# Layer 0 of a state-space and convolution network on one core: another order of the first steps, other places for the silus, one ScalarE table set for ln and exp

## Chip, cores and metric

The kernel runs on one core of a Trainium2 chip. The core has TensorE (PE in the profile; PEld is its weight load), VectorE (DVE), ScalarE (ACT), GpSimd (POOL) and SyncE (SP), which here issues nearly all DMAs. The metric is the device time of one execution in microseconds, lower is better.

## What is computed

Input x is 4 images of 512 channels by 32 by 32 points, all in float32. Layer 0 is a selective state-space mixer over the 1024 points of each image taken as tokens; layer 1 is a block of 3x3 convolutions with a spatial attention map. Both sit behind a group norm and a residual sum.

```python
x = x + _L0(_gn(x), ...)
x = x + _L1(_gn(x), ...)

# layer 0
xn = (x - mu) / sqrt(var + 1e-05) * ln_w + ln_b
xm, z = split(xn @ W_in)                       # 1024 channels each
xs = silu(causal_conv4(xm) + conv_b)
proj = xs @ W_x
dt = softplus(proj[..., :32] @ W_dt + b_dt)
Bm, Cm = proj[..., 32:48], proj[..., 48:]
A = -exp(A_log)
h = exp(dt * A) * h + (dt * xs) * Bm           # along the tokens, 16 states
y = sum_s(h * Cm) + xs * D_param
out = (y * silu(z)) @ W_out
```

## The kernel before

**Layer 0** goes through the batches b = 0 to 3. The 1024 channels of the mixer are 8 tiles of 128 (NDC); tokens come in 2 halves of 512 (NH). One *group* is a pair of channel tiles (index e) and one half (h): 8 groups a batch, 32 in all. A group runs 16 *units* (`unit`), one for each state s: ScalarE computes the decay exp(dt A) (`decay`, L832, two of 128 x 512), the input term comes either from ScalarE row scalings that TensorE turns (L844, L870; nine states, `B_ON_ACT`) or from a GpSimd product (L859; seven states), VectorE runs the recurrence (`tensor_tensor_scan`, L884), the product with C is GpSimd's (L906) except for four states of VectorE's (L900), and TensorE adds the states up in PSUM (L913). A group is opened by `delta` (step size dt: matmul L394 `pd`, bias L779, softplus L785, product with x on GpSimd L793, transposes and copies L809) and closed by `gate` (copies of y L936, transposes back L946, D x and the product with silu(z) on VectorE L953 and L956, store to `gd`).

While batch b goes through its groups, the next batch is prepared beneath: `norms` (group norm and layer norm over channels; its square roots are made as exp(-0.5 ln v), L458 and L463 for the group norm, L550 and L556 for the layer norm, with squares at L532 and matmuls at L539), `conv1` (projection to xm in three parts, four taps on ScalarE and VectorE, L639 and L648, then a silu of the whole 128 x 1024 tile, L657), `params` (`proj`, with B and C to DRAM `bcd` and back as broadcast tiles `cbc` and `bbc`). `gates` projects z, copies it out of PSUM (L707), applies silu (L711, 128 x 1024) and stores it to DRAM `szd`; `gate` loads it back as `szl` (one buffer) four units before its group ends.

Batch 0 has a version by halves, `conv1_half`: the first half's eight channel tiles are projected and convolved, the three last columns of each are kept in `tails`, group 0 can then start, and the second half follows beneath it, with small instructions at L687 for the columns that straddle the halves.

A filler runs under all this: `transform`, 32 pieces that prepare the 3x3 weights of layer 1 (GpSimd L1173 to L1193, ScalarE L1165 and L1166, loads of 192 KB and stores of 128 KB by SyncE). Eleven of them (PRM `t0`) come with priority -190, the others every 21.42 units (`tg`).

**The order** of all instructions of layer 0 is worked out when the kernel is built. `Plan.step` records an engine, an estimated duration, what is read and written, a priority (`prio`, in units: group n of batch b starts at (8b + n) x 16) and the ScalarE function table that is needed (`table`). `Plan.issue` then simulates the five engines: for each it takes, of the steps that can start soonest, the one with the lowest priority number; a step that needs another table is charged `LOAD` = 1.3 us, and only entered early if no urgent step of the present table waits. Steps marked `fill` may run up to 17.64 units (`AHEAD`) ahead. Each engine then executes its instructions strictly in that order. ScalarE's function tables are loaded by an instruction of their own (`ACT_TABLE_LOAD` in the profile, listed under the line that needs it), which the compiler puts in.

**Layer 1** (from L1260 on in the program, 2045 us in the profile) is not touched, apart from one thing: its group norms (`rsqrt`, L255 and L256) also use ln and exp.

```python
PRM = dict(..., m0=45.7, n0=50.77, q0=65.56, qg=5.2, c0=61.67, cg=6.03, e0=3.46, eg=4.75, dl=10.28, t0=11, tg=21.42)
"xs": 10, "win": 2, "yt": 1, "dt": 2, "dtx": 2, "dtxt": 2, "cbc": 5,
"sc": 2, "h": 4, "sz": 1, "bb": 3, "dbx": 4, "szl": 1, "wpr": 2, "res": 2,
```

These are the priorities and the buffers of each ring that the text speaks of; PSUM has two buffers `mm`, four `u` and two `y` besides.

Of the kernel before, what the change touches and what calls it, by code (L numbers as in the profile page):

```python
# [15 lines left out]
P = 128  # L16
# [14 lines left out]
PRM = dict(pg=0.53, kt=2, ke=1, ka=-0.68, fl=0, fi=4.6, m0=45.7, n0=50.77, nl=2.05, q0=65.56, qg=5.2, c0=61.67, cg=6.03, p0=112, e0=3.46, eg=4.75, g0=78.98, gg=9.04, o0=13.03, og=5.23, dl=10.28, t0=11, tg=21.42)  # L31
# [24 lines left out]
class Plan:  # L56
# [7 lines left out]
    def __init__(self, slots, in_order):  # L64
        self.slots, self.steps = dict(slots), []
        self.queues = {r: [] for r in in_order}
# [37 lines left out]
    def issue(self):  # L104
# [6 lines left out]
        while left:  # L111
# [32 lines left out]
            s.fn()  # L144
            if late:
                t += self.LOAD
                table = s.table
            clock[s.eng] = t + s.us
# [21 lines left out]
def mamba_then_pab_kernel(  # L170
# [31 lines left out]

    gm_sb = cpool.tile([P, P], F32, tag="gmat", name="gm_sb")
# [70 lines left out]
    with ExitStack() as l0:  # L274
# [6 lines left out]

        NT = L // P
# [41 lines left out]
        tails = wp.tile([P, NDC, 3], F32, tag="tails", name="tails")  # L324
# [7 lines left out]
        def dram_set(name, shape, n=B):  # L332
# [14 lines left out]
            ("xt", "u", "h", "cbc", "bb", "dbx", "sc"),  # L347
# [31 lines left out]
        xts, ready, xs, xh, dts = {}, {}, {}, {}, {}  # L379
        pieces = buf(None, None, "")  # L380
        tail = [buf(None, None, "") for d in range(NDC)]
# [19 lines left out]
        def norms(b, prio, lag=0.0):  # L401

            t = xts[b] = buf("xt", [P, NCC, L], f"xt_{b}")
            src = x[b].rearrange("(c p) h w -> p c (h w)", p=P)
            xin = [buf(None, None, "") for c in range(NCC)]
            step("SP", 0.0, lambda: t(), [], [], prio, holds=[t])
            for c in range(NCC):
                step(
                    "SP", 0.3, lambda c=c: nc.sync.dma_start(t()[:, c, :], src[:, c, :]),
# [29 lines left out]
            def mid():  # L439
# [19 lines left out]
                [pv], [stat], prio, "ln",  # L459
# [42 lines left out]
            by_chunk = by_token(NCC)  # L502
            for h, hs in enumerate(halves):
                prio += lag
# [8 lines left out]
                    prio, holds=[t],  # L513
                )
                for c in range(NCC):
# [6 lines left out]
                        [pmu], [by_half[h]], prio, holds=[t],  # L522
                    )
            pvars = []
            for h, hs in enumerate(halves):
                prio += lag
                pvar = buf("mm", [P, T], f"pvar_{b}_{h}")
                for c in range(NCC):
                    sq = buf("res", [P, T], f"sq_{b}_{h}_{c}")
                    step(  # L530
                        "ACT", 0.61,
                        lambda c=c, hs=hs, sq=sq: nc.scalar.activation(  # L532
                            sq(), t()[:, c, hs], AF.Square, bias=spl["nb"][:, c : c + 1]
                        ),
                        [by_half[h], stat], [sq], prio, holds=[t],
# [86 lines left out]
        def tap_weights(d):  # L622
            return [cw_sb[:, 4 * d + 3 - k : 4 * d + 4 - k] for k in range(4)]
# [1032 lines left out]
```

## Time and profile before

| what | us |
|---|---|
| median of 3 runs (lowest, highest) | 3085.72 (3081.79, 3090.05) |
| the profiled execution: its time, its span | 3085.98, 3084.2 |
| busy in the span: TensorE, VectorE, ScalarE, GpSimd | 2760.5, 2325.2, 1864.1, 2181.5 |
| softplus of group 0, of group 1 | 105.5, 200.7 |
| ends of the groups of batch 0 (`yt` copy, L936) | 242, 301, 361, 418, 487, 552, 614, 667 |
| of batch 1 | 721, 778, 835, 895, 968, 1032, 1096, 1148 |
| of batch 2 | 1201, 1259, 1312, 1376, 1449, 1513, 1577, 1630 |
| of batch 3 | 1683, 1741, 1794, 1842, 1897, 1945, 1997, 2045 |

Times within an execution count from the first instruction. Batches 0 to 2 take some 480 us each from one end of the last group to the next, batch 3 takes 415; the first group of all ends at 242. Layer 1 begins at 2045 and fills the other third, with TensorE busy 968.3 of the last 994 us.

A row of a group of instructions gives line, engine, operation, output and inputs, shapes, the count, then busy time and the mean of one in ns, then the engine's idle time just before them with what ended it. In a row of busy time by window each engine's microseconds stand with its count of instructions; PEclk is TensorE's granted clock.

### The profile page before, as it was taken

How to read it: one execution, taken by the hardware profiler on the slowest of the kernel's cores; microseconds unless marked ns; L12 is line 12 of the kernel's file. 1: busy time of each engine (PE TensorE's matmuls, PEld its weight loads, DVE VectorE, ACT ScalarE, POOL GpSimd, SP SyncE). 2: the span in 40 equal slices, each digit the busy share in tenths (PEclk: the TensorE clock that was granted, in tenths of full speed). 3: DMA queues.
4: the chain of work that ended last, by engine and by line, in shares of the span. 5: the costliest groups of instructions: out<-in, count | busy, mean ns of one | idle time of the engine just before them, and what ended most of it. 6: DMA issues, size and time to landing. Idle time of an engine off the chain costs nothing. (4 is left out here: it accounts for less than half of the span.)

```text
span 3084.2 us, 36053 instructions
## 1 busy us (share of the span) xinstructions
PE 2760.5 (90%) x11512; PEld 1625.3 (53%) x11512; DVE 2325.2 (75%) x3021; ACT 1864.1 (60%) x3218; POOL 2181.5 (71%) x1221
## 2 busy tenths in 40 slices
PE   4788789999879999879999978779999999999998
PEld 2245556656656666656656656544444444444444
DVE  3567999989999988999999899986275375447344
ACT  4578899998789999779999787741120030021000
POOL 6899988899988899998899999862151142224222
PEclk8899899999989999988999999999999999999999
DMA  6776645578745567755557755638178448628827
GB/s 170 216 208 197 178 143 164 171 210 255 230 138 163 165 204 238 236 176 158 174 167 238 237 184 151 148 123 307 54 259 314 163 165 315 256 76 313 309 86 259
DMA packets 410292, 610.49 MB, mean 198 GB/s; under 512 B 47832, under 2 KB 246744, under 8 KB 385528
## 3 DMA queue, kind: packets, MB, share of 16 engines
q1 hardware_dynamic: 401296, 593.67, 61.1%
q10 hardware_dynamic: 8648, 14.26, 1.3%
q8 instruction: 92, 1.51, 0.2%
q14 instruction: 96, 0.79, 0.1%
q0 software_dynamic: 160, 0.26, 0.0%
HBM read 511.09 MB, written 96.99 MB: 197 GB/s over the span
## 5 line engine op out<-in xcount | busy, mean ns | idle before, releaser
L906 POOL TENSOR_TENSOR da<-da,cbc 128x1024 f32<-128x1024 f32 x288 | 680.6, 2370 | 80.4 <-DVE da L884 50.7
L844 ACT ACTIVATE sc<-dtxt,bt_sb 128x256 f32<-128x256 f32 x1152 | 506.6, 497 | 70.6 <-PE u L870 70.1
L859 POOL TENSOR_TENSOR dbx<-dtx,bbc 128x1024 f32<-128x1024 f32 x224 | 529.1, 2373 | 20.1 <-PE y L913 7.0
L832 ACT ACTIVATE da<-dt,a_sb 128x512 f32<-128x512 f32 x576 | 395.4, 712 | 45.7 <-PE y L913 42.9
L884 DVE TENSOR_TENSOR_SCAN da<-da,carry_sb,u 128x512 f32<-128x512 f32 x288 | 357.6, 1263 | 34.5 <-PE u L870 34.5
L870 PE MATMUL u<-ident,sc 128*128 128x128 f32 x2304 | 345.8, 284 | 41.1 <-DVE da L884 26.0
L913 PE MATMUL y<-ident,da 128*128 128x128 f32 x2304 | 317.3, 282 | 53.2 <-POOL da L906 50.7
L913 PEld LDWEIGHTS y<-ident,da 128*128 128x128 f32 x2304 | 269.3, 145 | 155.6 <-POOL da L906 104.5
L884 DVE TENSOR_TENSOR_SCAN da<-da,u 128x512 f32<-128x512 f32 x288 | 348.6, 1210 | 2.6 <-PE u L870 2.4
L1468 PE MATMUL m_b<-uw_b,v_b 128*128 128x512 f32 x768 | 336.3, 595 | 8.8 <-DMA uw_b<-u_b 7.7
L870 PEld LDWEIGHTS u<-ident,sc 128*128 128x128 f32 x2304 | 277.2, 146 | 122.8 <-DVE da L884 34.7
L1468 PE MATMUL m_o<-uw_o,v_o 128*128 128x512 f32 x768 | 334.2, 595 | 4.3 <-DVE v_o L1387 4.1
L832 ACT ACTIVATE u<-dt,a_sb 128x512 f32<-128x512 f32 x448 | 297.6, 680 | 47.3 <-DVE da L884 27.6
L913 PE MATMUL y<-ident,dbx 128*128 128x128 f32 x1792 | 267.8, 289 | 61.2 <-DVE dbx L900 31.0
L913 PEld LDWEIGHTS y<-ident,dbx 128*128 128x128 f32 x1792 | 219.2, 149 | 135.0 <-issue 48.0
L394 PE MATMUL pxm<-xt,winc 128*128 128x345 f32 (+3 forms) x704 | 249.4, 498 | 29.3 <-DMA winc<-in_w_in_dram 12.9
L394 PE MATMUL pz<-xt,winc 128*128 128x512 f32 x512 | 240.3, 601 | 8.4 <-ACT sz L707 2.1
L1468 PEld LDWEIGHTS m_b<-uw_b,v_b 128*128 128x128 f32 x768 | 143.2, 190 | 195.0 <-issue 174.5
L1468 PEld LDWEIGHTS m_o<-uw_o,v_o 128*128 128x128 f32 x768 | 145.3, 190 | 190.1 <-issue 181.3
L906 POOL TENSOR_TENSOR dbx<-dbx,cbc 128x1024 f32<-128x1024 f32 x96 | 227.2, 2366 | 15.5 <-DVE dbx L884 7.5
L1518 PE MATMUL pat<-y_b,st 128*128 128x512 f32 x512 | 221.7, 593 | 0.1
L1476 ACT ACTIVATE e_b<-m_b 128x512 f32<-128x512 f32 x24 | 14.3, 597 | 307.9 <-PE m_b L1468 306.3
(233 smaller groups left out, 4543.1 us busy)
## 6 DMA issues: line engine op xcount, KB each, us to landing
cbc<-bcd SPq DMA_DIRECT2D x512, 256.0 KB, 3.7
uw_b<-u_b SPq DMA_DIRECT2D x96, 1024.0 KB, 5.1
uw_o<-u_o SPq DMA_DIRECT2D x96, 1024.0 KB, 4.8
bbc<-bcd SPq DMA_DIRECT2D x224, 256.0 KB, 3.9
u_b<-work SPq DMA_DIRECT2D x192, 128.0 KB, 2.7
u_o<-work SPq DMA_DIRECT2D x192, 128.0 KB, 3.3
winc<-in_w_in_dram SPq DMA_DIRECT2D x72, 256.0 KB, 3.6
szd<-sz SPq DMA_DIRECT2D x32, 512.0 KB, 4.1
```

The costliest lines, as they stand in the source:

```text
L394: lambda k=k, lhs=lhs, rhs=rhs: nc.tensor.matmul(p()[:, at : at + cols], lhs(), rhs(), start=(k == 0), stop=(k == n - 1)),
L832: nc.scalar.activation(t, dt()[:, j], AF.Exp, scale=a_sb[:, at : at + 1])
L844: nc.scalar.activation(sc()[:, k], dtxt()[:, k], AF.Copy, scale=bt[:, at, s : s + 1])
L859: lambda: nc.gpsimd.tensor_mul(hc(), dtx(), b_bc().to_broadcast([P, 2, T])),
L870: nc.tensor.transpose(u()[:, k * P : (k + 1) * P], sc()[:, k, j, :], ident)
L884: nc.vector.tensor_tensor_scan(ht, *((hc()[:, j], u()) if on_act else (u(), hc()[:, j])), carry_sb[:, j, s : s + 1] if h else 0.0, ALU.mul ...
L906: lambda: nc.gpsimd.tensor_mul(hc(), hc(), c_bc().to_broadcast([P, 2, T])),
L913: nc.tensor.matmul(y[j]()[:, k, :], hc()[:, j, k * P : (k + 1) * P], ident, start=(s == 0 and k == 0), stop=(s == NS - 1 and k == NK - 1), ...
L1468: nc.tensor.matmul(m[q], v[:, q, k, c, :], w[:, c, :], start=(c == 0), stop=(c == NCC - 1 and not extra),)
L1476: nc.scalar.activation(e, m[2], AF.Copy, scale=al / 2)
L1518: nc.tensor.matmul(pt, st[m][:, 2 * P * j + h : 2 * P * (j + 1) : 2], xb[m // 2][:, m % 2, :], start=(m == 0), stop=(m == NMC - 1),)
```

## The change

- **Tables.** `exp_set`, a preload of the set `natural_log_exp_and_others`, is issued at the kernel's start and by the plan each time that ScalarE comes back to exp; steps of ln now carry the table name "exp".
- **silu of z.** `gates` no longer applies it; z is stored as projected. `load_gate` loads it 11.5 units (`zl`) before its group ends, instead of 4, and its silu (128 x 1024, over both tiles of the pair) is run by the *next* group's `delta`.
- **One ScalarE step.** `delta`'s softplus step first runs a list of jobs: the silu of the last group's z and, in groups 5, 6 and 7 of a batch, the silu of two x tiles of the next batch; then softplus. The last two x tiles of a batch have a step of their own (`alone`). `gate` is recorded after the next group's `delta` (`end_group`). TensorE's transposes in `gate` now also wait for the z tile.
- **First steps.** x of batch 0 is loaded ahead of the plan; its norm goes by halves (`at_half`), with the squares in the `dt` and `dtx` buffers instead of the two of `res`; `conv1_half` becomes `conv1_first`, which takes the second half in two parts of 256 columns and projects three columns again instead of keeping `tails`; its silus come for four tiles at once in the second half. Priorities: norm -60 to -20, first convolutions -26 to -17, transforms -190 to -5.
- **Numbers.** `t0` 11 to 7, `tg` 21.42 to 18.5, `dl` 10.28 to 8.5, `e0` 3.46 to 6, `m0` 45.7 to 48; batch 1's convolutions use the spacing of the other batches.

```diff
-PRM = dict(..., m0=45.7, ..., q0=65.56, qg=5.2, ..., e0=3.46, ..., dl=10.28, t0=11, tg=21.42)
+PRM = dict(..., m0=48, ..., e0=6, ..., dl=8.5, t0=7, tg=18.5, zl=11.5, f1=1.5)
...
-            s.fn()
             if late:
                 t += self.LOAD
                 table = s.table
+                if table == "exp":
+                    self.exp_set()
+            s.fn()
...
+    def exp_set():
+        nc.scalar.preload_act_table_set("natural_log_exp_and_others")
+
+    exp_set()
...
+        first_x = xtp.tile([P, NCC, L], F32, tag="xt", name="xt_0", bufs=1)
+        for c in range(NCC):
+            nc.sync.dma_start(first_x[:, c, :], x[0, c * P : (c + 1) * P].rearrange("p h w -> p (h w)"))
...
+            at_half = [prio + (lag * h if b else 0.5 * h) for h in range(NH)]
...
-                    sq = buf("res", [P, T], f"sq_{b}_{h}_{c}")
+                    if b:
+                        sq = buf("res", [P, T], f"sq_{b}_{h}_{c}")
+                        sqt = lambda sq=sq: sq()
+                    else:
+                        if c % 2 == 0:
+                            sq = buf(("dt", "dtx")[h], [P, 2, T], f"sq_{b}_{h}_{c}")
+                        sqt = lambda sq=sq, c=c: sq()[:, c % 2]
...
+        def conv_part(b, d, w, at, end, prio, early=False):
...
+            step("ACT", 0.09 + n / 1000, ...)
+            def taps():
+                for k in range(1, 4):
+                    first = max(at, k)
+                    nc.vector.scalar_tensor_tensor(
+                        u()[:, first:end], p()[:, first - k - at + before : n - k + before],
+                        cw[k], u()[:, first:end], ALU.mult, ALU.add,
+                    )
+
+            step("DVE", 0.25 + n * 0.0042, taps, [p], mine, prio, holds=[u])
+
+        def silu(b, ds, hs=slice(0, L)):
+
+            hh = [h for h in range(NH) if hs.start < T * (h + 1) and hs.stop > T * h]
+
+            def each():
+                for d in ds:
+                    u = xs[b, d]()[:, hs]
+                    nc.scalar.activation(u, u, AF.Silu, bias=cb_sb[:, d : d + 1])
...
+        def alone(job, prio):
+            fn, us, bufs, holds = job
+            step("ACT", us, fn, [], bufs, prio, "silu", holds=holds)
...
-            step(
-                "ACT", 0.97, lambda: nc.scalar.activation(sz(), sz(), AF.Silu),
-                [], [sz], prio, "silu",
-            )
...
+            def softplus():
+                for fn, *_ in jobs:
+                    fn()
+                nc.scalar.activation(dt(), dt(), AF.Softplus)
+
+            step(
+                "ACT", 0.97 + sum(j[1] for j in jobs) + (1.3 if jobs else 0), softplus,
+                [], [dt, *(t for j in jobs for t in j[2])], prio, "softplus",
+                holds=[t for j in jobs for t in j[3]],
             )
...
+        def load_gate(b, e, h):
+
+            prio = (b * NDC + 2 * e + h) * NS + NS
+            hs = halves[h]
+            sz = szl[b, e, h] = buf("szl", [P, 2, T], f"szl_{b}_{e}_{h}")
+            step(
+                "SP", 0.3, lambda: nc.sync.dma_start(sz(), szd[b][e][:, :, hs]),
+                szds[b][2 * e : 2 * e + 2], [sz], prio - PRM["zl"], kb=512,
+            )
+            return lambda: nc.scalar.activation(sz(), sz(), AF.Silu), 1.0, [sz], []
...
-                step("PE", 4 * TR, turn, [yt], [p], prio + 2)
+                step("PE", 4 * TR, turn, [yt, sz], [p], prio + 2)
...
-        norms(0, -60)
+        norms(0, -20)
         for d in range(NDC):
-            conv1_half(d, 0, -26 + 0.1 * d)
-        params(0, -24, (0,))
+            conv1_first(d, 0, -17 + 0.1 * d)
+            alone(silu(0, [d], slice(0, T)), -17 + 0.1 * d)
+        params(0, -16, (0,))
...
-            transform(u, src, k % NPC, -190 if k < PRM['t0'] else PRM['tg'] * (k - PRM['t0']))
+            transform(u, src, k % NPC, -5 if k < PRM['t0'] else PRM['tg'] * (k - PRM['t0']))
...
+                jobs = []
+                if b or n > 1:
+                    prev = b * NDC + n - 1
+                    jobs.append(load_gate(prev // NDC, prev % NDC // NH, prev % NH))
+                if b + 1 < B and n > 4:
+                    jobs.append(silu(b + 1, (2 * n - 10, 2 * n - 9)))
+                delta(b, e, h, at + n * NS - PRM["dl"] if b or n else -15, jobs)
+                end_group()
...
+                if b + 1 < B and n + 1 == NDC:
+                    alone(silu(b + 1, range(6, NDC)), at + PRM["c0"] + PRM["cg"] * NDC)
+                    params(b + 1, at + PRM["p0"])
...
+        alone(load_gate(*ended[0][:3]), B * NDC * NS - 2)
+        end_group()
```

## The prediction

> **What bounds the kernel now.** I read the busy slices first, to see where each engine fills up, then busy time in windows laid at the ends of the groups (a group is one step of 2 channel tiles by 512 tokens with its 16 states; its end is the `yt` copy, L936), then the ScalarE groups for table loads, then the timeline of the first 120 us.
>
> ```profile
> ACT  4578899998789999779999787741120030021000
> POOL 6899988899988899998899999862151142224222
> ```
>
> Both engines are near full up to slice 26 (2045 us, the end of the last group of layer 0), and idle most of the time in layer 1, which TensorE bounds. The change has to pay before 2045 us.
>
> ```profile
> core 0: us, PE busy (x) PEld busy (x) DVE busy (x) ACT busy (x) POOL busy (x), PEclk, DMA share, GB/s
> 0.00:125.00 125.00, 71.00 (x148) 29.84 (x149) 36.85 (x66) 51.71 (x85) 98.78 (x105) 0.85 0.67 186
> 125.00:205.00 80.00, 68.36 (x208) 30.73 (x207) 53.93 (x78) 56.90 (x89) 70.03 (x63) 1.00 0.77 220
> 205.00:418.00 213.00, 168.81 (x930) 119.47 (x928) 187.33 (x248) 184.71 (x319) 206.25 (x115) 0.91 0.60 179
> 418.00:614.00 196.00, 178.94 (x928) 123.75 (x929) 185.38 (x271) 185.79 (x309) 171.82 (x91) 0.97 0.56 165
> 614.00:895.00 281.00, 252.79 (x1369) 172.08 (x1366) 251.93 (x325) 238.89 (x426) 272.00 (x150) 0.96 0.73 217
> 895.00:1096.00 201.00, 179.32 (x929) 124.54 (x930) 190.30 (x277) 190.82 (x314) 172.93 (x92) 0.96 0.55 162
> 1096.00:1376.00 280.00, 253.84 (x1360) 174.54 (x1359) 251.33 (x324) 237.55 (x424) 272.11 (x148) 0.95 0.71 217
> 1376.00:1577.00 201.00, 181.41 (x938) 124.56 (x937) 189.38 (x276) 189.78 (x313) 172.86 (x94) 0.96 0.53 159
> 1577.00:1842.00 265.00, 237.05 (x1324) 162.16 (x1324) 237.77 (x293) 230.69 (x411) 260.23 (x139) 0.98 0.72 217
> 1842.00:2045.00 203.00, 160.21 (x960) 114.23 (x958) 199.53 (x264) 149.29 (x283) 182.37 (x85) 0.97 0.54 146
> ```
>
> There are three regimes. The **start** (to 205 us, five units done) fills no engine but GpSimd, and that with weight transforms. The **light** groups (205:418, 614:895, 1096:1376, 1577:1842) belong to GpSimd: 1010.6 of 1039 us busy, 28.4 idle. The **heavy** groups (418:614, 895:1096, 1376:1577), where the next batch's convolution runs, belong to ScalarE and VectorE: 566.4 and 565.1 of 598 us, GpSimd only 517.6, so 80.4 idle. In the last window VectorE has 199.5 of 203.
>
> ```profile
> L832 ACT ACT_TABLE_LOAD x76 | 97.5, 1283 | 1.4
> L785 ACT ACT_TABLE_LOAD x32 | 41.1, 1283 | 0.6
> L711 ACT ACT_TABLE_LOAD x28 | 35.9, 1283 | 0.5
> L657 ACT ACT_TABLE_LOAD x24 | 30.8, 1283 | 3.3 <-DVE xs L648 2.6
> ```
>
> Each load takes 1.283 us of ScalarE and nothing around it: 76 reloads of exp have 1.4 us of idle before them together. With the smaller lines (L695, L226 and the ln/exp pairs) there are 185, or 237 us. By window, the heavy ones hold 28, 28 and 27.
>
> ```profile
> 46.37 1.58 ACT L532 ACTIVATE sq<-xt,gnb_l 128x512 f32<-128x512 f32 x2 [0.39 <-PE pvar L539]
> 51.99 1.28 ACT L556 ACT_TABLE_LOAD   x1
> 62.05 15.97 PE L394 MATMUL pxm<-xt,winc 128*128 128x512 f32 x32 [11.48 <-DMA winc<-in_w_in_dram]
> 105.46 1.06 ACT L785 ACTIVATE dt<-dt 128x1024 f32<-128x1024 f32 x1
> 114.89 2.49 POOL L793 TENSOR_TENSOR dtx<-dt,xs 128x512 f32<-128x512 f32 x2
> ```
>
> The start is a chain: squares that trade two buffers with TensorE, ln and exp with a load each, a projection that waits for its weights, a softplus whose product waits 8.4 us (106.5 to 114.9) in GpSimd's queue behind transforms.
>
> **Loads after the change.** Three per group (silu, softplus, back to exp) for 30 groups, 90; the lone pair of x silus of each batch, 2 x 3 = 6; some 12 in the start; 2 at the last gate; none in layer 1. That is 110, 75 fewer, 96 us of ScalarE. Where another engine sets the pace they are worth nothing, so I price by regime.
>
> The Trainium skill says otherwise of a switch ("ScalarE: Activation LUTs", What ACT_TABLE_LOAD costs): 1283 ns plus a drain of some 1380, 2.66 us in all. The rows above show the first half and no drain; by the page the 75 loads would be 200 us of ScalarE, and the heavy windows would still stop at VectorE.
>
> **Start.** (a) Group norm: one exp load on the path goes (22.49), -1.3. The four squares of a half get buffers of their own (in dt and dtx): first square 36.4, last pvar matmul 50.6; a half needs 8 of the 16 matmuls, so its ln can start near 45, not 50.7; the exp load (1.28) goes too. Then multiply and affine of half 0 trail by one step each, as now, and pxm can start near 50, since winc (now -17, transforms -5) is no longer issued behind transforms. Against 62.05: -12 (bounds -4, if TensorE's early matmuls stay spaced at 0.85 us, to -14). (b) Eight first convolutions: winc reloads still pace them; the tail copies go: -3 (0 to -6). (c) dtx behind transforms: seven pieces still precede it; half of 8.4: -4 (0 to -8.4). (d) Second halves, 125 to 205: VectorE's L687 tails go. They take 20.6 us there for 24 instructions of 1 to 3 columns; they are replaced by 48 taps of 256 columns for 24 of 512. A 341-column tap is 569 ns and a 512-column one 738, so 256 is about 485: 48 x 0.485 = 23.3 against 17.7 + 20.6, -15 on VectorE; table loads 10 to about 5, -6 on ScalarE. TensorE holds 68.4 of 80, so not all counts: -10 (0 to -20). The x loads go ahead of two transform loads that SyncE issued at 1.17, one microsecond sooner; but the fourth chunk's statistics wait at 18.62 behind `a_sb`, whose load arrives by ScalarE's queue, so that gain is 0. Sum **-29** (-4 to -48); group 0 would end near 213, not 241.9.
>
> **GpSimd's transforms.** One piece is 12.0 us (three of 1.82 and nine of 0.73). Before, 12 of 32 began by 205 us, under a start that left GpSimd free. After, seven have priority -5 and the next are at 0 and 18.5, so about 9 fit: three pieces, 36 us, move into the loop. Spacing falls from 21.42 to 18.5 units. The share landing in heavy groups goes into their 80 us of idle; what lands in light ones lengthens them one for one, since only 28 us are idle there. **+20** (+8 to +36).
>
> **Heavy groups.** 83 loads become about 33 (three groups of three, plus two, in each): -64 us of ScalarE. VectorE is next, at 565.1 of 598: at 97.5% of its time the windows would be 580. **-18** (0, if VectorE's waits stay, to -33).
>
> **The long ScalarE step.** Its cover is the four `u` buffers, two units of about 3.6 us, 7.2. With two x silus it takes 1.28 + 1.06 + 2 x 1.15 + 1.28 + 1.06 + 1.28 = 8.3 us, nine times: about 1 us over each. Without, 6.0, covered. It now also waits, in ScalarE's order, for the z tile: behind it stand every sc and decay, hence scans, hence GpSimd. `szl` has one buffer; in the trace its load is issued 3 to 7 us after the store of the tile before (gd 311.37, szl 314.78), lands 5.0 later (median, at most 7.2), and would be needed 8.5 units before the group's end, at about 329 there and 450 for the one issued at 442.0. Slack 3 to 9 us. In SyncE's queue the earlier szl load, held until that store has landed, stands ahead of cbc and bbc loads; their five and three buffers, more than a unit's worth each, hide a wait of some 3 us. Without that cover GpSimd's products would wait as long, inside the bound. **+4** (0 to +20; a gain is excluded, no engine gets less work by it).
>
> **Elsewhere.** The image norm's exp load (2052.28) is on the path into layer 1, -1.3. The last z silu with two loads, 3.6 us, falls in a group where ScalarE idles half the time: 0, to +3.6 without that cover. The later layer-1 ln/exp loads (6 x 1.28) lie under TensorE's matmuls; nothing, up to -3.
>
> Sum: -29 + 20 - 18 + 4 - 1.3 = **-24**; I take -26, as fewer loads in light windows also help where ScalarE is 54 of 54 us (667:721). The profiled run took 3085.98 (span 3084.2 plus 1.8 around it), the median is 3085.72, equal here. Forecast **3060**.
>
> **Rivals.**
> 1. *Slower: the long step stalls ScalarE.* For: slack of 3 us where gates run late, and a load that lands up to 2.2 us past its median; ScalarE's order holds all behind it. Against: the planner knows the wait and delays the step, and softplus comes 8.5 units early. The sum without the step's +4 is -30, spread over 30 groups, so it decides from 1.3 us uncovered in each (+39, less 30: 3095), which is a z tile late by 2.5 us, as 1.2 of the plain step's cover are free; at 2 us each it is +60 - 30: about 3116. Chance 0.25.
> 2. *No difference.* Transforms take back what the start gives (+36) and heavy windows stay at VectorE's waits: -29 + 36 - 5 - 1 = 0: 3086. For: GpSimd's work is the same, and it rules the light groups. Chance 0.09.
> 3. *More.* The start gives its 48, transforms fit into heavy idle (+8), VectorE fills (-33), no stall: -74: 3012. For: all four slacks are in the windows. Against: they must come together. Chance 0.16.
> 4. *The set isn't kept:* exp still gets a load of its own after each preload. Then about 40 returns to exp cost 1.283 twice, +51 us of ScalarE; part falls where ScalarE has room, so I count half: -26 + 25, about 3085. The Trainium skill ("ScalarE activation tables: per-element evaluation and per-set limits", Table sets in the compiler and the runtime) has the back end place loads itself, by longest run, which speaks for it; no row of this trace shows a preload. Chance 0.04.
>
> **Numbers.** The forecast (3040 to 3076) has 0.46. A measurement here tells 0.3%, 9.3 us. Faster by more: 0.46 + 0.16 + 0.03 = 0.65. Within: 0.10. Slower: 0.25. The range 3005 to 3115 leaves out the far ends of rivals 1 and 3; the forecast's own is 3040 to 3076.
>
> **What would show it.** Loads about 110, none by L550/L556/L255; pxm starting near 50; group 0 ending near 213; heavy windows near 195 us (580 + 4, in three) with VectorE at 97% and GpSimd busier; light groups longer by about 1 us each (20 over 18). Rival 1: ScalarE idle before the z silu, released by the szl transfer. Wrong throughout if the start doesn't shorten: then the moved transforms alone decide.

## The result, and the profile after

The changed kernel takes 3112.60 us (median of 5 runs, 3104.28 to 3120.52) against 3081.79 (3076.57 to 3090.05) for the kernel before on the same chip: ratio 1.0105, interval 1.0089 to 1.0121. It is about 1% slower. Forecast were 3060 and a range of 3005 to 3115 with faster as the likeliest sign; the time lies inside the range and the sign was wrong.

Two lengths carry all that follows. The **start** is the time of the first `yt` copy that ends group 0; the **loop** runs from there to the `yt` copy of the last group of layer 0. Before: start 241.9, loop 1802.6, end 2044.5. After: start 193.5, loop 1875.2, end 2068.7. The start is 48.4 shorter, the loop 72.6 longer. Layer 1 takes the rest, 1039.7 before and 1042.0 after.

The busy slices of the changed kernel, ScalarE and GpSimd:

```profile
ACT  4678887897787888687898777852030030030000
POOL 6989998999988999989899998863152142224222
```

ScalarE, mostly at 8 or 9 before, now stands at 7 or 8 in the loop; GpSimd is as full as it was. Busy time by window, laid at the changed kernel's group ends (start, then three heavy windows with the light one between the first two):

```profile
core 0: us, PE busy (x) PEld busy (x) DVE busy (x) ACT busy (x) POOL busy (x), PEclk, DMA share, GB/s
0.00:193.50 193.50, 150.90 (x540) 87.12 (x541) 105.83 (x187) 106.78 (x180) 159.70 (x143) 0.96 0.67 186
...
385.40:583.40 198.00, 177.15 (x932) 124.54 (x932) 185.63 (x271) 161.52 (x287) 177.94 (x101) 0.97 0.56 166
583.40:871.30 287.90, 252.14 (x1356) 166.92 (x1356) 246.99 (x319) 233.92 (x423) 277.94 (x153) 0.96 0.71 216
871.30:1076.10 204.80, 181.98 (x939) 125.12 (x938) 191.96 (x281) 167.92 (x296) 178.00 (x101) 0.97 0.56 162
...
1367.20:1572.00 204.80, 179.00 (x939) 122.46 (x938) 192.09 (x281) 167.88 (x295) 177.74 (x101) 0.98 0.53 162
```

In the heavy windows ScalarE fell by 22 to 24 us each (185.5, 191.4 and 190.0 in the same groups before). The windows became longer: 198.0, 204.8 and 204.8 for 195.9, 201.6 and 201.2. No engine is full in them. The light window 583:871 is 287.9 for 280.3, and GpSimd is busy in 277.9 of it.

The table loads of the changed kernel:

```profile
L206 ACT ACT_TABLE_LOAD x40 | 51.3, 1283 | 3.1 <-issue 1.7 <-PEq L1681 0.7
L786 ACT ACT_TABLE_LOAD x32 | 41.1, 1283 | 0.5
L935 ACT ACT_TABLE_LOAD x32 | 41.1, 1283 | 5.0 <-DMA szl<-szd 4.5
L675 ACT ACT_TABLE_LOAD x6 | 7.7, 1283 | 1.9 <-DVE xs L661 1.9
```

They are 110: returns to exp at the preload's line L206, softplus, silu of z, silu of x; none for ln. The kernel before has 189 of them, 242.5 us: the prediction's 185 leave out four of its small lines. So 79 loads went, 101 us of ScalarE. ScalarE waited 6.0 us in all for z tiles, 4.5 of them before a load. The timeline of the start, the rows that answer to those of before:

```profile
30.95 0.72 ACT L550 ACTIVATE sq<-xt,gnb_l 128x512 f32<-128x512 f32 x1 [5.88 <-DVE xt L529]
40.58 7.13 PE L402 MATMUL pxm<-xt,winc 128*128 128x512 f32 x16 [0.15 <-ACT xt L593]
91.95 1.06 ACT L786 ACTIVATE dt<-dt 128x1024 f32<-128x1024 f32 x1
93.08 2.49 POOL L798 TENSOR_TENSOR dtx<-dt,xs 128x512 f32<-128x512 f32 x2 [1.08 <-ACT dt L786]
```

The first projection starts 21.5 us sooner, group 0's softplus 13.5, its product on GpSimd 21.8, now waiting for the softplus alone. What grew in the loop shows in ScalarE's waits (what it waited for; us in total, times, longest), 193 to 2069 us of the changed kernel:

```profile
engine line waited for: us in total, times, longest us
ACT sc L849 <- PE u L875: 133.5, 74, 8.6
ACT da L837 <- PE y L918: 60.8, 47, 5.7
```

The same two of before, 241 to 2045 us:

```profile
ACT sc L844 <- PE u L870: 69.8, 66, 3.4
ACT da L832 <- PE y L913: 42.9, 45, 2.9
```

ScalarE stands before its row scalings until TensorE's transposes have emptied an `sc` buffer, which in turn need a free `u`. Together the two waits grew by 81.6 us, most of the time that ScalarE no longer spends on table loads.

### The profile page after: what moved, and what is told of

Its sections match the earlier page's. It is cut to its first block, busy times and chain, and to the rows that moved or that the text cites. A ratio compares the mean times of both kernels' runs of the same rounds, so it can differ in the third digit from the quotient of the medians.

```text
span 3110.7 us, 36162 instructions
## 1 busy us (share of the span) xinstructions
PE 2775.2 (89%) x11576; PEld 1643.6 (53%) x11576; DVE 2296.5 (74%) x3021; ACT 1763.7 (57%) x3139; POOL 2184.5 (70%) x1221
## 4 chain that ended last, share of the span: by engine, by line
PE 36%; DVE 13%; ACT 4%; DMA 3%; POOL 3%; issue 2%; SPq 0%; DVEq 0%; POOLq 0%; ACTq 0%
PE m_o L1503 10%; PE m_b L1503 8%; PE pat L1553 7%; DVE da L889 4%; PE y L918 2%; DVE u L889 2%; PE psc L1380 2%; DVE dbx L889 2%; PE po L402 1%; DMA uw_b<-u_b 1%; PE u L875 1%; ACT sc L849 1%; DVE dbx L905 1%; PE pt L1359 1%; DVE xs L661 1%
## 5 line engine op out<-in xcount | busy, mean ns | idle before, releaser
L911 POOL TENSOR_TENSOR da<-da,cbc 128x1024 f32<-128x1024 f32 x288 | 680.1, 2366 | 105.6 <-DVE da L889 57.5
L918 PE MATMUL y<-ident,da 128*128 128x128 f32 x2304 | 324.0, 286 | 59.9 <-POOL da L911 58.0
L837 ACT ACTIVATE u<-dt,a_sb 128x512 f32<-128x512 f32 x448 | 298.8, 680 | 38.7 <-DVE da L889 23.0
L918 PEld LDWEIGHTS y<-ident,dbx 128*128 128x128 f32 x1792 | 218.6, 149 | 130.8 <-POOL dbx L911 39.5
L402 PE MATMUL pxm<-xt,winc 128*128 128x344 f32 (+4 forms) x768 | 251.0, 469 | 23.2 <-DVE xs L661 9.7
L402 PE MATMUL pz<-xt,winc 128*128 128x512 f32 x512 | 245.0, 597 | 11.5 <-DVE xs L661 3.6
L1503 PEld LDWEIGHTS m_b<-uw_b,v_b 128*128 128x128 f32 x768 | 143.7, 190 | 195.9 <-issue 181.6
L661 DVE SCALAR_TENSOR_TENSOR xs<-pxm,cw_sb,xs 128x341 f32<-128x341 f32 (+8 forms) x288 | 163.6, 569 | 59.4 <-ACT xs L652 52.2
```

The source lines that it names most:

```text
L402: lambda k=k, lhs=lhs, rhs=rhs: nc.tensor.matmul(p()[:, at : at + cols], lhs(), rhs(), start=(k == 0), stop=(k == n - 1)),
L661: nc.vector.scalar_tensor_tensor(u()[:, first:end], p()[:, first - k - at + before : n - k + before], cw[k], u()[:, first:end], ALU.mult, ...
L837: nc.scalar.activation(t, dt()[:, j], AF.Exp, scale=a_sb[:, at : at + 1])
L911: lambda: nc.gpsimd.tensor_mul(hc(), hc(), c_bc().to_broadcast([P, 2, T])),
L918: nc.tensor.matmul(y[j]()[:, k, :], hc()[:, j, k * P : (k + 1) * P], ident, start=(s == 0 and k == 0), stop=(s == NS - 1 and k == NK - 1), ...
L1503: nc.tensor.matmul(m[q], v[:, q, k, c, :], w[:, c, :], start=(c == 0), stop=(c == NCC - 1 and not extra),)
```

## The experiments

Each run stood beside the kernel before on the same chip (medians 3078 to 3082 us). Start, loop and end come from one profiled execution each; executions of one kernel lie up to 16 us apart (the changed kernel, 3104 to 3120), so a difference of a few microseconds between two loops says little.

| kernel | start | loop | end | time, us | ratio to before, interval |
|---|---|---|---|---|---|
| before | 241.9 | 1802.6 | 2044.5 | 3081.79 | |
| after | 193.5 | 1875.2 | 2068.7 | 3112.60 | 1.0105 (1.0089, 1.0121) |
| b_pieces0 | 273.7 | 1798.8 | 2072.5 | 3105.56 | 1.0073 (1.0058, 1.0088) |
| a_pieces0 | 219.1 | 1864.8 | 2083.8 | 3123.68 | 1.0133 (1.0114, 1.0152) |
| b_noload | 237.3 | 1796.2 | 2033.5 | 3071.37 | 0.9966 (0.9953, 0.9979) |
| a_noload | 194.0 | 1862.8 | 2056.8 | 3093.04 | 1.0049 (1.0029, 1.0068) |
| c_sep | 194.1 | 1858.1 | 2052.1 | 3097.55 | 1.0060 (1.0041, 1.0078) |
| c_sepB | 192.1 | 1844.1 | 2036.1 | 3075.65 | 0.9988 (0.9978, 0.9997) |
| a_dl | 193.4 | 1864.6 | 2058.0 | 3096.31 | 1.0058 (1.0039, 1.0078) |
| a_t11 | 238.8 | 1831.1 | 2069.8 | 3111.22 | 1.0109 (1.0086, 1.0132) |
| b_t7 | 228.5 | 1838.5 | 2066.9 | 3104.02 | 1.0080 (1.0056, 1.0103) |
| c_sepBt | 242.2 | 1805.4 | 2047.6 | 3084.98 | 1.0014 (0.9999, 1.0029) |
| b_np | 240.3 | 1777.5 | 2017.7 | 3056.56 | 0.9925 (0.9903, 0.9947) |
| a_np | 209.6 | 1801.9 | 2011.5 | 3048.49 | 0.9903 (0.9880, 0.9926) |
| a_xsep | 194.5 | 1872.5 | 2067.0 | 3109.78 | 1.0090 (1.0075, 1.0105) |
| a_b10 | 196.3 | 1834.0 | 2030.3 | 3069.47 | 0.9958 (0.9946, 0.9971) |
| b_b10 | 242.5 | 1786.8 | 2029.3 | 3063.01 | 0.9932 (0.9915, 0.9950) |
| a_num_b10 | 194.6 | 1836.6 | 2031.2 | 3067.67 | 0.9954 (0.9938, 0.9970) |
| c_best | 195.9 | 1834.3 | 2030.2 | 3065.92 | 0.9956 (0.9939, 0.9974) |
| c_bestx | 197.8 | 1809.9 | 2007.8 | 3043.73 | 0.9875 (0.9856, 0.9894) |

**1. Work taken out, order kept** (b_pieces0, a_pieces0: GpSimd's 385 us of transform arithmetic; b_noload, a_noload: silu and softplus replaced by functions that need no other table, so that 164 of 189 and 109 of 110 loads go, 210 and 140 us). Every engine keeps the order of its kernel.

```diff
-eng.tensor_add(plus(), ends()[:, 1:3], ends()[:, 0:1].to_broadcast([P, 2, 3, QC]))
+plus()                                  # pieces0: likewise for the other eleven
...
-dst, o()[:, q - 1] if q in (1, 2) else b()[:, 0:2, q // 3 * 2]
+dst, ends()[:, 0:2, q // 3 * 2]         # pieces0: all stores read the loaded tile
...
-AF.Silu ... AF.Softplus
+AF.Identity ... AF.Exp                  # noload
```

> The kernel before, in its own order on every engine, with GpSimd's arithmetic of the 32 weight pieces left out (385 us of GpSimd; loads, ScalarE scalings and stores stay, the weights of layer 1 are raw taps). Theory G (GpSimd's total work rules the time up to the end of layer 0): the light groups, where GpSimd was 97% busy, become shorter by some 15 to 20 us each window, heavy ones hardly: 60 to 90 us less in all, near 3000. Rival R (GpSimd's share is a symptom, VectorE and the order pace the light groups too): less than 30 us.

> The changed kernel in its own order with the same arithmetic left out. Theory G: the start's 48 us count once GpSimd's pieces no longer follow into the loop; against the kernel before without pieces it is 15 to 30 us faster (48 less some 27 of waits behind the long ScalarE step). Rival R (the long ScalarE step alone costs the loop its 72 us): still 15 us or more slower than the kernel before without pieces.

> The kernel before in its own order, with identity for silu and exp for softplus, so that some 170 of 185 table loads vanish (about 218 us of ScalarE) and nothing else moves; the values are other ones. If loads set the pace of the heavy groups, as predicted: 40 us or more less (18 in heavy windows as forecast, more elsewhere). If VectorE, GpSimd and the fixed order set it: 15 us or less.

> The changed kernel in its own order, no table loads in layer 0 after the first (108 of 110 vanish, 139 us of ScalarE; identity for silu, exp for softplus). The long step shrinks from 6.0 or 8.3 us to 2.1 or 4.4. If the long step starves VectorE beyond the cover of two units: 25 us or more less, and VectorE's waits for decays and turned inputs fall back to the kernel before's. If not: 10 us or less.

The loops moved by 3.8 and 10.4 us without GpSimd's transforms, by 6.4 and 12.4 without the loads. The loop of after stays 66.0 and 66.6 us above that of before in both pairs. So neither the loads nor GpSimd's busy time *as executed* makes the difference. For the loop b_pieces0 fell to its rival R, b_noload to the smaller of its two ranges; a_noload, some 17 us faster than the changed kernel by the ratios, lies between its two. a_pieces0 is 18 us slower than b_pieces0, as its rival R had it. No expectation had it that both starts grow with this edit (last section). In a_pieces0 the chain of work that ended last, by engine, and GpSimd's largest group say where the time is:

```profile
PE 49%; DVE 23%; ACT 13%; DMA 7%; issue 4%; POOL 2%; SPq 1%; ACTq 0%; DVEq 0%; POOLq 0%
...
L911 POOL TENSOR_TENSOR da<-da,cbc 128x1024 f32<-128x1024 f32 x288 | 680.2, 2366 | 342.7 <-DVE carry_sb L894 133.0
```

GpSimd idles 342.7 us before its products (105.6 in the changed kernel) and has 2% of the chain (3%), and still the loop is hardly shorter. The other engines keep the sequence that was worked out for a GpSimd with transforms; worked out anew without them, the loops are 25.1 and 73.3 us shorter (b_np and a_np below). From here on the order is worked out anew in each kernel. No run was planned anew without the table loads, so what they cost there stays open.

In the expectations G is the theory that GpSimd's transforms cost the loop (by their places in the plan, after these runs), P that the combined ScalarE step does, N that the loop's numbers do; T is G with the start's gain put down to the same transforms, R that the first steps' new order made the start shorter.

**2. Parts of the change undone** (c_sep: both silus back at their old places, z's gate load four units ahead; c_sepB: also dl, e0, m0 and batch 1's convolution spacing; a_dl: dl alone; a_t11: the transforms' t0 and tg).

```diff
-jobs.append(load_gate(...)); jobs.append(silu(b + 1, (2 * n - 10, 2 * n - 9)))
+step("ACT", 0.97, ..., AF.Silu ...)  # c_sep: in gates; alone(silu(b, [d]), prio) in conv1
...
-m0=48, e0=6, dl=8.5, zl=11.5, conv1 at c0 + cg * d
+m0=45.7, e0=3.46, dl=10.28, conv1 of batch 1 at 65.56 + 5.2 * d   # c_sepB
+dl=10.28, zl=13.28                                                # a_dl
-t0=7, tg=18.5
+t0=11, tg=21.42                                                   # a_t11
```

> The changed kernel with its silus put back where they were before (z's in the gates, x's after each convolution, the gate's load four units before the group's end); its start, its exp set and its numbers stay. Theory P (the combined ScalarE step spoils the planned order): the loop, first to last group end, falls from 1875 to 1800-1820 us, first group still at about 194, so about 3040-3060 in all. Theory N (the loop's numbers dl, e0, m0, spacing of batch 1): the loop stays at 1865-1885, time 3100-3120. Theory G (the transforms that moved out of the start, by the places they take in the plan): the same 1865-1885, time 3100-3120.

> The kernel of the run before this one, and with the loop's numbers of the kernel before as well (dl 10.28, e0 3.46, m0 45.7, batch 1's convolutions at 65.56 + 5.2 d); only the start, the exp set and the pace of the transforms remain of the change. Theory P: about as the run before, loop 1800-1820, time 3040-3060. Theory N: now the loop is back to 1800-1815 while the run before was not; time 3040-3055. Theory G: still 1850-1885, time 3090-3120, since nine transforms instead of twelve precede the loop and come every 18.5 units.

> The changed kernel with dl 10.28 again instead of 8.5 (and the z tile's load earlier by the same 1.78 units). Theory N, if dl is the number: the loop falls from 1875 to 1800-1830, time 3045-3075. Theory P and theory G: 1865-1885, time 3100-3125. If any change of the planned order moves the loop by ten and more microseconds either way, it lands outside all three.

> The changed kernel with the transforms' numbers of the kernel before: eleven early, then one every 21.42 units. Theory G: start longer by some 0-25 us, loop shorter by 35-65, since four more pieces precede it and they come as sparsely as before: time 3070-3100. Theory P and theory N: loop within 15 of 1875, time 3095-3125.

No theory alone was right: c_sep and c_sepB ended between the ranges of P, N and G, a_dl outside all of them, as its text had left open, and a_t11's loop fell as G had it, though its start grew by 45.3 instead of 0 to 25. The silus back give 17.1 us of loop, the numbers 14.0 more (dl alone gave 10.6), the old transforms 44.1. And a_t11 brought the surprise of the study: with the old transforms' numbers, the *reordered* start is 238.8, as long as the old one. GpSimd between group 0's softplus and its end, a_t11 first, then the changed kernel:

```profile
91.30:238.80 147.50, 111.29 (x443) 71.60 (x442) 71.65 (x120) 85.31 (x157) 139.75 (x111) 0.86 0.74 205
```

```profile
92.00:193.50 101.50, 85.71 (x384) 57.95 (x383) 66.17 (x115) 68.09 (x120) 94.29 (x71) 0.93 0.67 185
```

The softplus comes at the same time in both, 91.3 and 92.0 us. From there GpSimd is busy 139.8 of 147.5 and 94.3 of 101.5 us. Three transforms of 12.0 us (12 begun by 200 us for 9) are 36 of the 45 us of GpSimd work between them. With 12 transforms GpSimd fills the rest of the new start; with 9 it does not seem to set it, for in a_np (part 3), without any, the same stretch is not shorter (its softplus comes at 102.5):

```profile
102.50:209.60 107.10, 88.59 (x387) 60.24 (x386) 66.41 (x115) 73.06 (x127) 53.74 (x25) 0.89 0.68 194
```

**3. Transforms and first steps apart** (b_t7: the kernel before with t0 7 and tg 18.5; c_sepBt: c_sepB with t0 11 and tg 21.42; b_np and a_np: both kernels planned and built without the transforms' GpSimd work, their stores reading the loaded tile as in pieces0).

```diff
-t0=11, tg=21.42
+t0=7, tg=18.5                                     # b_t7; c_sepBt the reverse
...
-step(name, 1.76, ...) x3 ... step(name, 2.28, columns, ...)
+step(name, 0.02, ...) x3 ... step(name, 0.02, ...)  # b_np, a_np, without the arithmetic
```

> The kernel before with two numbers of the change alone: seven transforms early instead of eleven, then one every 18.5 units instead of 21.42. Theory T (the start got shorter because four transforms, some 48 us of GpSimd, left it, and the loop pays for them): first group ends at 190-210 instead of 242, the loop grows from 1803 to 1835-1850, time 3070-3090. Rival R (the reordered first steps made the start shorter): first group at 225-242, loop 1803-1850, time 3085-3130.

> The kernel before, planned as if the GpSimd work of the 32 transforms took no time, and without that work (their loads, ScalarE scalings and stores stay; layer 1 reads the untransformed weights). Unlike the earlier run without this work, the order of all engines is worked out anew. Theory T (in-order engines: the places that transforms take in the plan cost the loop): first group at 190-215, loop 1660-1740 instead of 1803, time 2870-2980. Rival (VectorE and ScalarE bound the loop whatever GpSimd does): loop 1780-1805, time 3020-3060.

> The changed kernel, planned and built without the GpSimd work of the transforms in the same way. Theory T: its start is no shorter than that of the kernel before in the same state (within 15 us, since the transforms made the difference), and its loop stands 15-45 us above, by the long ScalarE step and the loop's numbers. Rival: start shorter by 35-50 us, loop above by 60-75 as with the transforms.

> The changed kernel with silus, the loop's numbers and the transforms' numbers of the kernel before; what remains of the change are the reordered first steps and the exp set. Theory T: first group at 235-242, loop 1790-1808, time 3070-3085. Rival R: first group at 194-215, loop 1795-1810, time 3035-3060.

b_t7 came out in every range of rival R, c_sepBt in those of theory T or at their edge (242.2, 1805.4 and 3084.98), so neither theory of the start is right alone: fewer transforms alone give 13.4 us (228.5), the reordered first steps alone nothing (242.2), both together 49.8 (192.1). In the old order of the first steps the stretch from group 0's softplus to its end hardly answers to GpSimd: 136.4 us with 125.7 of GpSimd work, 124.8 with 90.8 (b_t7). In the new one it does, 151.7 with 139.7 (c_sepBt), 100.8 with 94.9 (c_sepB). b_np fell to its rival: without the transforms' 385 us the loop is 25.1 us shorter, not 63 to 143. a_np's loop stands 24.4 us above it, as T had it, but its start is 30.7 us shorter, which T had excluded. For the loop the terms are nearly additive:

| | transforms as before | transforms as after | difference |
|---|---|---|---|
| loop as before, first steps old | 1802.6 | 1838.5 (b_t7) | +35.9 |
| loop as before, first steps new | 1805.4 (c_sepBt) | 1844.1 (c_sepB) | +38.7 |
| silus and numbers of the change | 1831.1 (a_t11) | 1875.2 (after) | +44.1 |
| silus and numbers, difference | +25.7 to +28.5 | +31.1 | |

Without any transform work the same silus and numbers cost 24.4 (1777.5 to 1801.9). Of the 32 transforms, 12 are begun before group 0 ends with the old numbers and 9 with the new, in all six kernels of the table, so 20 or 23 run in the loop (t0 says four fewer early; it is three). The 20 cost 25.1 us in the old loop (before less b_np) and 29.2 in the new (a_t11 less a_np); the three more cost 35.9 to 44.1. A transform of 12.0 us costs 1.3 to 1.5 us on the average of the 20, and the next ones 12 to 15 us each, their full time or more. t0 and tg were always moved together, so the three more transforms and their closer pace are not told apart.

Where the loop pays, by windows laid at each kernel's own group ends (light: the first three groups and the three stretches of five that follow the heavy ones; last: the last four groups; GpSimd's work as transforms + all other):

| | light | heavy | last | GpSimd in light | GpSimd in heavy |
|---|---|---|---|---|---|
| before | 1001.6 | 598.8 | 202.1 | 166.7 + 806.5 | 74.4 + 444.0 |
| b_t7 | 1029.0 | 603.8 | 205.7 | 170.1 + 823.8 | 106.4 + 424.6 |
| c_sepBt | 1003.3 | 598.4 | 203.7 | 168.7 + 810.0 | 72.5 + 443.5 |
| c_sepB | 1049.5 | 589.5 | 205.0 | 175.0 + 847.8 | 102.3 + 410.7 |
| a_t11 | 1010.5 | 615.1 | 205.4 | 167.6 + 807.7 | 73.8 + 445.2 |
| after | 1057.0 | 607.6 | 210.6 | 168.8 + 835.3 | 108.3 + 425.4 |

The three more transforms run in the heavy windows, but 19 to 33 us of GpSimd's other work goes from there into the light ones, which are full, and those grow by 27 to 47 us. Silus and numbers cost elsewhere: 17 to 18 us of their 26 to 31 are in the heavy windows.

**4. What pays it back** (a_xsep: x's silus out of the step, z's kept in it; b10: state 7's input term from GpSimd to ScalarE and TensorE; a_num_b10: that with c_sepB's numbers and zl 13.28; c_best: c_sepB with it; c_bestx: c_best with the x pairs kept in the step before softplus).

```diff
-B_ON_ACT = (0, 2, 4, 6, 8, 10, 12, 14, 15)
+B_ON_ACT = (0, 2, 4, 6, 7, 8, 10, 12, 14, 15)
```

> The changed kernel with the silus of x taken out of the ScalarE step and put back after each convolution; z's silu stays in it. Whichever of the two makes the step dear: if the x pairs (8.3 us against two units), the loop falls by 12-20 from 1875 as it did with both taken out, heavy groups above all, time 3090-3100; if z's silu, in every group, the loop stays within 6 of 1875 and the time is 3105-3125.

> The changed kernel with state 7's input term made by ScalarE and TensorE (ten states instead of nine), as state 6's is: 32 GpSimd products of 2.37 us fewer, 76 us; 256 ScalarE row scalings of 0.50 us more, 127 us, and 256 transposes. Theory T (GpSimd's work, as planned, is what the four moved transforms overfill): loop from 1875 to 1810-1845, time 3050-3080. Rival (ScalarE and VectorE bind the loop beside GpSimd): the 127 us land on ScalarE, loop 1865-1930, time 3100-3165.

> The same state moved in the kernel before, whose ScalarE has 100 us less to give. Theory T: GpSimd is filled, not overfilled, so nothing is gained there, and ScalarE is overfilled in the heavy groups: loop 1803-1860, time 3080-3140. Rival (GpSimd binds both kernels alike): loop 1760-1790, time 3040-3070.

> The changed kernel with state 7 moved and the loop's numbers of the kernel before (dl 10.28, e0 3.46, m0 45.7, batch 1's convolutions at 65.56 + 5.2 d). By theory T the numbers give 11-14 more than the state alone: loop 1797-1832, time 3037-3067, faster than both kernels. Rival: within 15 of the changed kernel's 1875.

> The changed kernel's first steps, seven early transforms and exp set; silus and loop's numbers of the kernel before; state 7's input term on ScalarE and TensorE. If what the four moved transforms cost is GpSimd's overfill, relieving it is worth as much here as in the changed kernel (41), not as little as in the kernel before (16): first group at 192-196, loop 1844 - 41 = 1800-1815, time 3030-3045, faster than both kernels by 1.2% or more. If the 41 came from ScalarE's freed time, which this kernel has given up, the loop gains 16 or less: 1825-1845, time 3055-3075.

> The same with the silu of x pairs kept in the ScalarE step before softplus, z's silu in the gates. If z's silu in that step is what costs, as the difference of the earlier runs has it, this stands within 8 us of the run before it; if the x pairs cost, it is 10 to 20 slower.

The expectations of b10 counted eight row scalings a state; there are four, so ScalarE takes half of the 127 us or less (its busy time rose by 46.8 us in a_b10). a_b10 came as theory T had it, b_b10 as its rival. The gain in loop was 41.2 us in the changed kernel (ScalarE busy 1810.5 us afterwards) and 34.2 from c_sepB to c_bestx (1843.6; the x pairs moved as well), but 9.8 from c_sepB to c_best (1872.5) and 15.8 in the kernel before (1910.7). So c_best came out in the second of its two branches, the one of the smaller gain: relieving GpSimd alone does *not* buy the moved transforms back there. That ScalarE must have the time free is the reading that fits the four; the gains do not fall evenly with its busy time, and no run frees ScalarE alone. By that reading the fewer table loads leave room that the change did not use.

As for the step, a_num_b10 and c_bestx differ in z's silu only (in the step with its load 13.28 units ahead, or in the gates with the load 4 ahead): 1836.6 against 1809.9, and their ratio intervals lie apart. With x's silus outside, a_xsep against c_sep, it is 1872.5 against 1858.1. z's silu in the step, with its earlier load, therefore costs 14 to 27 us. The x pairs, which make the step longest, cost nothing that shows: 2.7 us from a_xsep to the changed kernel, within the scatter, and a gain of 24.4 from c_best to c_bestx, outside both of c_bestx's expectations. ScalarE's and VectorE's waits in a_num_b10, 195 to 2008 us:

```profile
DVE pyb L965 <- PE pyb L958: 17.4, 9, 11.2
...
ACT sc L849 <- PE u L875: 112.2, 63, 7.3
ACT da L837 <- PE y L918: 39.8, 39, 3.3
...
ACT szl L935 <- DMA szl<-szd: 7.2, 8, 3.0
```

The same stretch of c_bestx:

```profile
DVE pyb L970 <- PE pyb L963: 2.3, 3, 1.4
...
ACT sc L853 <- PE u L879: 69.2, 50, 5.3
ACT da L841 <- PE y L922: 60.1, 46, 4.0
```

z's tile itself holds ScalarE for 7.2 us in 8 waits. The wait before the row scalings is 43.0 us less in c_bestx, that for room in `y` 20.3 more, and VectorE's wait for the turned y of `gate`, whose transposes also wait for z, 15.1 less. How z's place in the order brings that wait about, step by step, was not followed further. c_bestx beats both kernels: 1.25% faster than before by its ratio, 2.2% below the changed kernel by the medians (of different chips).

## Why the prediction was wrong

**Loads.** Right for the changed kernel: 110 of 1.283 us, 33 of them in the heavy windows, no load for ln, the set kept (rival 4 fell). The count before was 189, not 185, so 79 fewer and not 75. No drain shows around them: the four rows have 10.5 us of idle before 110 loads, and the next instruction of ScalarE starts 0.012 us after a load (median). The drain of some 1.38 us that the Trainium skill gives for a switch ("ScalarE: Activation LUTs", What ACT_TABLE_LOAD costs) would be 152 us, an estimate from the page; the rows decide.

**Start, -29 (-4 to -48).** Measured -48.4, at the bound. By parts it was no sum that came out: (a) -21.5 for -12 (the projection at 40.6), (b) +8.0 for -3 (from there to the softplus 51.4 us, 43.4 before), (c) -8.3 for -4, (d) -26.6 for -10 (from dtx to the end of the group). And the reason was wrong. I had read that the start fills no engine but GpSimd, and then priced other engines' work. c_sepBt and b_t7 show that those parts are worth nothing (242.2) until three transforms leave; then they are worth 36 (b_t7 to c_sepB). Start and transforms are one term, not two: net of what the loop pays, c_sepB against c_sepBt ends 11.5 us earlier, and a_t11 against the changed kernel 1.1 later.

**GpSimd's transforms, +20 (+8 to +36).** That three transforms more come into the loop was right; the price was not. In place it is +36 to +44 for 46 us more of GpSimd work in the loop (1673.7 before, 1720.0 after). I had let part of it vanish in the heavy groups' 80 us of idle. The transforms did land there (74.4 us before, 108.3 after), but GpSimd's other work moved on into the light windows, which with the old silus and numbers grow by 46.2 us for it (c_sepBt to c_sepB) while the heavy ones shrink by 8.9. The step that failed is this overlap: idle time of an engine was taken as room, with no look at what would be pushed out of its place.

**Heavy groups, -18 (0 to -33).** This and the next step turned the sign: together they were to give 14 us of loop and cost 26 to 31 (table above). The failed step here is that fewer loads on ScalarE make the heavy windows shorter. Relieved by 22 to 24 us a window, ScalarE gave nothing, and the windows grew by 2 to 4 us. VectorE was to become the bound at 97.5% of its time; it stayed at 94% (185.6 of 198.0, 192.0 of 204.8). With the old transforms and the same relief they are 615.1 us for 598.4 (a_t11, c_sepBt). With the order kept, taking 210 us of loads out of the kernel before shortens its loop by 6.4 us: a microsecond of ScalarE is worth some three hundredths of one there. A busy share of 95% on two engines was read as a bound; in these runs it was none.

**Long ScalarE step, +4 (0 to +20).** With the numbers that I priced at nothing (dl, e0, m0, batch 1's spacing) it is +24 to +31; z's silu alone 14 to 27, the numbers 14.0 from c_sep to c_sepB. I looked at the step's length and its x pairs, which cost nothing that shows, and at the z tile's transfer, which came in time (6.0 us of waits for 32 tiles). dl was listed among the changes and given no price at all; returning it alone gave 10.6 us of loop, 1.0105 to 1.0058 in the ratio. What it does shows in VectorE's wait for ScalarE's decays in the loop, here before and after:

```profile
DVE dbx L884 <- ACT u L832: 17.8, 16, 2.4
...
DVE dbx L889 <- ACT u L837: 40.4, 11, 5.2
```

With x's silus out of the step it is still 43.4 (a_xsep); with dl back at 10.28 it is 0.9 (a_dl) and 1.8 (a_num_b10), and without silus in the step, at dl 8.5, it is 19.1 (c_sep). So this wait goes with dl 8.5 and z's silu in the step together, and a_dl's loop gains 10.6 of its 39.5 us. The failed step is the cover: the plain step of 6.0 us was called covered by the four `u` buffers, and dl was taken over at no price.

**Elsewhere, -1.3.** Layer 1 took 2.3 longer, within the scatter.

**The sum.** -48 + 41 + 31 is +24 (41 is c_sepB's loop less that of before, 31 the changed kernel's less c_sepB's), the end of layer 0 at 2068.7 for 2044.5. The terms were -29, +20, -18, +4. The time came out where rival 1 had put it (3095 to 3116), but only in part by its mechanism, and that is luck: the step does hold VectorE up, but by no late z tile, and some three quarters of the loop's loss (41 + 14 of 73) come from transforms and numbers. Rival 2's reason, that the transforms take back what the start gives, is what b_t7 and c_sepB show.

**What stays open.** The last terms of the order do not add: numbers gave 14 with the silus back but nothing with the silus in the step and state 7 moved (a_b10 1834.0, a_num_b10 1836.6, 4.6 above its expected range), and x pairs 2.7 in one pair and 24.4 in another. By these misfits a new plan moves the loop by some 10 us or more of its own (an estimate), so a part's price below that is not settled by these runs.

## What to carry to other kernels

In a kernel whose engines run a list worked out beforehand, price a moved step by what it pushes out of its place: 20 transforms cost 25 us and the next three, at a closer pace, 36 to 44, paid in windows other than those where they run. Do not count time freed on an engine as time gained: ScalarE was busy 100 us less in the changed kernel and its loop was longer; moving one state's GpSimd product onto ScalarE then gave 41 us, against 16 in the kernel before. And separate the parts by a small table of runs, both ways round, since a part may pay only together with another: the reordered first steps gained 0 or 36 us by the number of transforms beside them.

## What the runs showed of the hardware that was not expected

Less work made the start longer: without the transforms' arithmetic and in the same order, it grew from 241.9 to 273.7 us in b_pieces0. Waits up to the end of group 0, first in b_pieces0:

```profile
POOL dtx L793 <- ACT dt L785: 112.7, 1, 112.7
...
PE pxm L394 <- DMA winc<-in_w_in_dram: 37.4, 7, 14.6
...
SPq L1200 <- DMA work<-in_w_bottom_dram: 53.8, 25, 5.3
SPq L1160 <- DMA u_b<-work: 44.0, 40, 4.4
```

The same in the kernel before, where dtx has no wait for the softplus and L1200's wait for loads is 4.6 us:

```profile
PE pxm L394 <- DMA winc<-in_w_in_dram: 12.9, 3, 11.5
...
SPq L1160 <- DMA u_b<-work: 10.0, 10, 2.2
```

The transforms' transfers do not run ahead for want of GpSimd's arithmetic; they lag: by 100 us 18 loads and 56 stores of theirs are issued, for 21 and 68 in the kernel before. In this run every store reads the loaded tile. SyncE's queue stands at stores (L1200) until a load has landed and at loads (L1160) until stores have, and the projection's weights stand in the same queue: their sixth load goes at 99.6 us, for 86.8. TensorE waits 24.5 us longer for weights, and group 0's softplus comes 13.7 us later (119.2 for 105.5), for which GpSimd now stands idle. So the rows put the longer start down to where this run's stores read from, not to GpSimd's missing work; a run that separates the two was not made. b_np has the same stores (52.6 and 25.4 us of such waits), so its start of 240.3 does not show that the old start would be no shorter without transforms.
